# Second layer of the paired expert tiles: sums taken from PSUM, and three of four Strassen sums moved behind the scatter

## The chip, the cores and the metric

The kernel runs on one core of one Trainium2 chip. The metric is the device time of one execution in microseconds (us). Before the change three runs gave 2141.28, 2142.96 and 2143.67 us, a median of 2142.96 us. The profiled execution, from which all durations below are taken, took 2142.86 us; the part of it that the profile covers (its span) is 2140.9 us.

## The reference, cut to what matters

The model block is a cross attention (32 samples, 112 tokens of 256 features, 375 context rows) followed by a mixture of 8 experts. The change touches only the mixture's second layer. Its reference, shortened:

```python
xf = x.reshape(T, D)                                   # T = 3584 tokens, D = 256
gate_scores = softmax(xf @ gate_w)                     # 8 experts
topk_scores, topk_idx = top_k(gate_scores, 2)          # two experts for each token
topk_scores = topk_scores / sum(topk_scores)
h = gelu(einsum('td,edf->etf', xf, w1) + b1[:, None])  # F = 1024
y = einsum('etf,efd->etd', h, w2) + b2[:, None]
out = einsum('kt,ktd->td', topk_scores.T, y[topk_idx.T, tok])
x = x + tanh(g_ffn) * out
```

Everything is in float32. The kernel computes each token only for its two experts.

## The kernel before, in words

**Stages.** Up to about 1705 us the kernel does the attention and, for each finished slab of 128 tokens, routes the tokens: it writes each token's normalised row twice (once for each expert) into a DRAM buffer `xg` sorted by expert. From about 1705 to 2006 us it works through that buffer in *pairs*, 256 rows of one expert at a time (two blocks of 128 rows, b = 0 and 1). Rows that do not fill a pair are done from 1988 us to the end in *singles* of 128 rows, with plain products. This text deals with the pairs, t = 0 to 20. Pair 0 is done plainly; pairs 1 to 20 use a Strassen-Winograd scheme: the 2x2 block product of (rows) x (weights) needs 7 block products in place of 8, at the price of sums and differences of blocks before and after.

**One iteration, in the order in which the loop (L1563 to L1585) issues it.** All five engines run lists written out in this order (`tc.manual_schedule`), so each engine meets its own instructions in exactly this sequence:

1. `hidden_pair(t)`: seven products of the first layer, each of 8 matmuls (L1057), in the order 1, 6, 7, 5, 4, 2, 3, into tiles of the PSUM pool `ps_m`, which has 4 buffers. ScalarE copies product 1 (L1067); VectorE adds the other products into the tile `h` with seven adds, L1068, L1069, L1071, L1072, L1073, L1075 and L1076; ScalarE applies gelu (L1064).
2. `fetch_first(t + 1)`: SyncE issues the loads of the next pair's first-layer weights (L934). Each weight tile has one buffer, so that a load waits for the products of pair t that read it. The loads are conditional: they are left out when pair t + 1 has the same expert as pair t.
3. `turn_rows(t + 1)`: TensorE transposes the next pair's rows (L969) into a `ps_m` tile, ScalarE copies it to `xsT` (L973).
4. `rows_sums(t + 1)`: four GpSimd sums of 128x128 (L985) for the next pair's first layer.
5. `pieces_of(6)`: up to six pieces of leftover routing work, mostly on VectorE; it is used up by pair 8.
6. `hidden_sums(t)`: the four GpSimd sums of 128x512 for the second layer of pair t (L1094 and L1095): v0 = a21 + a22, a21 = a11 - a21 in place, v1 = v0 - a11, v2 = a12 - v1.
7. `second_pair(t - 1)`: seven products of the second layer of the pair in front (L1114), four into the PSUM tile `ps_ya`, which read a11, a12, a22 and v0, then three into `ps_yb`, which read a21, v1 and v2. ScalarE makes the scaled bias `by` (L1128) and copies the whole of `ps_ya` to the SBUF tile `q` (L1130). VectorE forms the result `y` from `q` and `ps_yb` in six adds (L1131, L1134 to L1138) and two multiply-adds, one for each block (L1140).
8. `out_pair(t - 1)`: GpSimd issues two indirect DMAs (L1018) that add the rows of `y` to the output in DRAM, one for each block. The last sum (v2, L1095) stands between the two.
9. `fetch_second(t)`: SyncE issues the loads of the second-layer weights of pair t (L951), which wait for the products of pair t - 1; then `fetch_rows(t + 3)` (L881) and, while there are any, one routing scatter to `xg` on GpSimd (L682).

Two facts of this order matter. VectorE meets the `y` adds of pair t - 1 just before the first-layer adds L1068 to L1076 of pair t + 1. And since `ps_m` has four buffers, used in the order of the products, product 2 takes the buffer of product 6, which is free once L1068 has run, and the transpose takes that of product 5, free once L1072 has run.

Of the kernel before, what the change touches and what calls it, by code (L numbers as in the profile page):

```python
# [8 lines left out]
F32 = mybir.dt.float32  # L9
I32 = mybir.dt.int32  # L10
AF = mybir.ActivationFunctionType
ALU = mybir.AluOpType
# [11 lines left out]
def kernel(  # L24
# [20 lines left out]
    nc = tc.nc  # L45

    P = 128
# [69 lines left out]
    for e in range(E):  # L117
# [35 lines left out]
    sums = {  # L153
        tag: [const.tile([P, E + 4], F32, name=f"sums{tag}_{n}") for n in range(4)] for tag in "abc"
    }
# [19 lines left out]
    if True:  # L175
# [641 lines left out]
        found = {}  # L817
# [54 lines left out]
        xs, xsT, xt, hid, hs, psy, ys, wt, bias = {}, {}, {}, {}, {}, {}, {}, {}, {}  # L872
# [143 lines left out]
        def add_rows(t, b, y):  # L1016

            add = nc.gpsimd.indirect_dma_start(  # L1018
                out=outf,
                out_offset=bass.IndirectOffsetOnAxis(  # L1020
                    ap=xs[t][:, b, D + 1 : D + 2].bitcast(I32), axis=0
                ),
                in_=y,
                in_offset=None,
                compute_op=ALU.add,
            )
            if b == 0 and "loose" in found:

                tc.add_manual_dep(
                    add.ins,  # L1030
                    found.pop("loose").name,
                    mybir.DependencyInfo(mybir.DependencyClass.Sync, mybir.DependencyReason.DATA),
                    reason="the same tokens",
                )
            return add

        def combine(t):
            n = 2 if t == 0 else 1
            y = found["tiles"].tile([P, 2, D], F32, tag="y", name=f"y_{t}")
            for b in range(n):  # L1040
                nc.vector.tensor_tensor(y[:, b], psy.pop((t, b)), bias[t][1], ALU.add)
                nc.vector.tensor_scalar(y[:, b], y[:, b], xs[t][:, b, D : D + 1], None, ALU.mult)  # L1042
                add_rows(t, b, y[:, b])


        def hidden_pair(t):


            h = hid[t] = found["tiles"].tile([P, NF, 2, P], F32, tag="h", name=f"h_{t}")
            x, v = xsT[t], xt[t]  # L1050
            H = NF // 2
            h11, h12, h21, h22 = (h[:, i : i + H, b, :] for i in (0, H) for b in range(2))

            def product(n, w, r):
                ps = ps_m.tile([P, H, P], F32, tag="m", name=f"ps_h_{t}_{n}")
                for c in range(H):
                    nc.tensor.matmul(  # L1057
                        ps[:, c, :], lhsT=wt[w][:, c * P : (c + 1) * P], rhs=r, start=True, stop=True
                    )
                return ps  # L1060

            def gelu(lo):
                for f in range(lo, lo + H):
                    nc.scalar.activation(h[:, f], h[:, f], AF.Gelu, bias=bias[t][0][:, f : f + 1])  # L1064

            add = nc.vector.tensor_tensor
            nc.scalar.copy(h11, product(1, "11", x[:, 0, 0]))  # L1067
            add(h12, product(6, "s2", v[:, 1]), h11, ALU.add)  # L1068
            add(h21, product(7, "s3", v[:, 2]), h12, ALU.add)  # L1069
            ps = product(5, "s1", v[:, 0])  # L1070
            add(h22, ps, h21, ALU.add)  # L1071
            add(h12, ps, h12, ALU.add)  # L1072
            add(h21, product(4, "22", v[:, 3]), h21, ALU.add)  # L1073
            gelu(H)
            add(h11, product(2, "12", x[:, 1, 0]), h11, ALU.add)  # L1075
            add(h12, product(3, "s4", x[:, 1, 1]), h12, ALU.add)  # L1076
            gelu(0)

        def hidden_sums(t):


            h, H = hid[t], NF // 2
            v = hs[t] = [
                found["tiles"].tile([P, H, P], F32, tag=f"hs{n}", name=f"hs{n}_{t}", bufs=1)
                for n in range(3)
            ]
            a11, a12, a21, a22 = (h[:, i : i + H, b, :] for b in range(2) for i in (0, H))
            sub = ALU.subtract
            for o, l, r, op in (
                (v[0], a21, a22, ALU.add),  # L1090
                (a21, a11, a21, sub),
                (v[1], v[0], a11, sub),
            ):
                nc.gpsimd.tensor_tensor(o, l, r, op)  # L1094
            last = lambda: nc.gpsimd.tensor_tensor(v[2], a12, v[1], sub)  # L1095
            if t > 1:
                found["last_sum"] = last
            else:
                last()

        def second_pair(t):


            h, v, H = hid[t], hs[t], NF // 2
            a11, a12, a21, a22 = (h[:, i : i + H, b, :] for b in range(2) for i in (0, H))
            b21, b22 = (wt["b2x"][:, :, i * P : (i + 1) * P] for i in range(2))
            tiles = found["tiles"]

            def products(name, parts):
                ps = ps_s.tile([P, 2, 512], F32, tag="s", name=f"ps_{name}_{t}")[:, 0, :]  # L1110
                ps = ps.rearrange("p (n d) -> p n d", d=P)
                for n, (w, r) in enumerate(parts):
                    for c in range(H):
                        nc.tensor.matmul(  # L1114
                            ps[:, n, :],
                            lhsT=w[:, c, :],
                            rhs=r[:, c, :],
                            start=(c == 0),
                            stop=(c == H - 1),
                        )  # L1120
                return ps

            y = tiles.tile([P, 2, D], F32, tag="y", name=f"y_{t}")
            q = tiles.tile([P, 4, P], F32, tag="q", name=f"q_{t}", bufs=1)
            u = tiles.tile([P, 2, P], F32, tag="u", name=f"u_{t}", bufs=1)
            by = tiles.tile([P, 2, D], F32, tag="by", name=f"by_{t}", bufs=1)
            for b in range(2):
                nc.scalar.mul(by[:, b], bias[t][1], xs[t][:, b, D : D + 1])  # L1128
            ps = products("ya", ((a11, wt["b11"]), (a12, b21), (a22, wt["t4"]), (v[0], wt["t1"])))
            nc.scalar.copy(q, ps)  # L1130
            nc.vector.tensor_tensor(y[:, 0, :P], q[:, 0], q[:, 1], ALU.add)  # L1131
            ps = products("yb", ((a21, wt["t3"]), (v[1], wt["t2"]), (v[2], b22)))
            add = nc.vector.tensor_tensor
            add(u[:, 0], ps[:, 1], q[:, 0], ALU.add)  # L1134
            add(u[:, 1], ps[:, 0], u[:, 0], ALU.add)
            add(y[:, 1, :P], u[:, 1], q[:, 2], ALU.add)
            add(y[:, :, P:], u, q[:, 3].unsqueeze(1).to_broadcast([P, 2, P]), ALU.add)
            add(y[:, 0, P:], ps[:, 2], y[:, 0, P:], ALU.add)  # L1138
            for b in range(2):
                nc.vector.scalar_tensor_tensor(  # L1140
                    y[:, b], y[:, b], xs[t][:, b, D : D + 1], by[:, b], ALU.mult, ALU.add
                )
            found["rows_out"] = y

        def out_pair(t):

            y = found.pop("rows_out")
            one = add_rows(t, 0, y[:, 0])
            last_sum = found.pop("last_sum", None)
            if last_sum:  # L1150
                last_sum()
            other = add_rows(t, 1, y[:, 1])
            if last_sum:
                tc.declare_no_dep(other.ins, one.ins, reason="rows of other tokens")
                found["loose"] = one.ins

# [147 lines left out]
        def do(parts):  # L1304
            for part in parts:
                part()
# [13 lines left out]
        ps = ps_m.tile([P, 4 * KD], F32, tag="m", name="ps_ln")  # L1320
# [53 lines left out]
        for n in range(LAST):  # L1374
# [46 lines left out]
            if nb < B:  # L1421
# [12 lines left out]
                if m in (6, 7) and nb + 2 < B or n == 1:  # L1434
                    u = m - 4 if m > 1 else 1
# [103 lines left out]
        r, _ = route_parts(g, nc.vector)  # L1539
# [23 lines left out]
        for t in range(1, PAIRS):  # L1563
            hidden_pair(t)
            fetch_first(t + 1)
            turn_rows(t + 1, nc.scalar.copy if t > 1 else None)
            if t + 1 < PAIRS:
                rows_sums(t + 1)
            pieces_of(6)
            hidden_sums(t)  # L1570
            if t > 1:
                second_pair(t - 1)
                out_pair(t - 1)
                fetch_second(t)
            else:
                second_plain(1)
                combine(0)
            if t + AHEAD == EARLY:
                pieces_of(len(todo))
                do(outgoing)  # L1580
                del outgoing[:]
            fetch_rows(t + AHEAD)
            if outgoing:
                outgoing.pop(0)()
# [65 lines left out]
```

## Time and profile before

| what | before |
|---|---|
| median of 3 runs | 2142.96 us |
| profiled execution | 2142.86 us, span 2140.9 us |
| TensorE busy | 2090.6 us, 98% of the span |
| VectorE busy | 1392.8 us, 65% |
| ScalarE busy | 1199.6 us, 56% |
| GpSimd busy | 963.3 us, 45% |
| `y` adds L1136, 128x128 | 20 times; 291 ns shortest, 1344 ns median, 1364 ns longest |
| `y` adds L1137, 128x256 | 20 times; 413 ns shortest, 1483 ns median, 1489 ns longest |
| `y` adds L1134, 128x128, one input in PSUM | 20 times; 279, 292 and 293 ns |
| copy of `ps_ya`, L1130, 128x512 | 20 times; 567 ns median |
| GpSimd sums L1094, 128x512 | 1262 to 1317 ns median |
| scatter L1018 on GpSimd | 60 times; 1552 ns median; 4.0, 5.7 and 7.8 us from issue to landing |

The engines in the profile are PE (TensorE's matmuls), PEld (its weight loads, which overlap the matmuls), DVE (VectorE), ACT (ScalarE), POOL (GpSimd) and SPq (SyncE's queue, which issues loads). In a timeline row the columns are the start in us from the beginning of the span, the length in us, engine, line of the kernel, operation, output and inputs, and in square brackets how long the engine had been idle and what ended that. In the list of waits a row says which engine and line waited for which, then the total in us, how often, and the longest.

### The profile page before, as it was taken

The numbers are of one execution on the slowest core, as the hardware profiler recorded it, in microseconds if no ns is written. First come the engines' busy times: TensorE is split into PE (matmuls) and PEld (weight loads), VectorE is DVE, ScalarE is ACT, GpSimd is POOL, SyncE is SP. The second block draws the span as 40 slices with busy tenths as digits, with TensorE's granted clock in tenths as the row PEclk, the third lists the DMA queues.
The fourth block names the chain that finished last, engine by engine and source line by source line (L and its number), as shares of the span: only waits on it lengthen the run. The fifth ranks groups of instructions, "written<-read, shape, count | busy, mean of one in ns | idle before, by whom it ended". The sixth has DMA issues, their size and how long they took to land. (4 is left out here: it accounts for less than half of the span.)

```text
span 2140.9 us, 44362 instructions
## 1 busy us (share of the span) xinstructions
PE 2090.6 (98%) x16232; PEld 1645.9 (77%) x16232; DVE 1392.8 (65%) x2985; ACT 1199.6 (56%) x2817; POOL 963.3 (45%) x1412
## 2 busy tenths in 40 slices
PE   9999999999999999999999999999999998999998
PEld 5777777777777777777777777777777888988887
DVE  6667676767676767676767676766767478666211
ACT  5666565656665666656666666665655443433433
POOL 4432323343345645553536443643323286766312
PEclk9999999999999999999999999999999999999999
DMA  6693000010012212222112211210002476598773
GB/s 149 187 319 103 18 13 18 13 30 18 18 44 63 67 55 58 61 67 58 55 55 65 65 55 55 68 54 6 6 6 73 134 196 179 161 298 267 191 212 64
DMA packets 201027, 193.89 MB, mean 91 GB/s; under 512 B 25856, under 2 KB 170824, under 8 KB 200680
## 3 DMA queue, kind: packets, MB, share of 16 engines
q1 hardware_dynamic: 188344, 174.65, 27.4%
q0 software_dynamic: 11328, 15.33, 3.8%
q8 instruction: 130, 2.13, 0.4%
q10 hardware_dynamic: 1136, 1.05, 0.2%
q14 instruction: 89, 0.73, 0.1%
HBM read 168.20 MB, written 65.76 MB: 109 GB/s over the span
## 5 line engine op out<-in xcount | busy, mean ns | idle before, releaser
L492 ACT ACTIVATE ex<-ex,rc 112x487 f32<-112x487 f32 x512 | 331.1, 694 | 329.4 <-DVE rc L490 326.4
L468 DVE TENSOR_REDUCE nmx<-ps_s 112x2 f32<-112x974 f32 x256 | 288.0, 1167 | 311.5 <-PE ps_s L458 310.5
L478 ACT ACTIVATE ex<-ps_s,nmx 112x487 f32<-112x487 f32 x512 | 337.1, 666 | 159.8 <-DVE nmx L468 157.4
L499 PEld LDWEIGHTS ps_t<-ident,ex 112*122 112x122 f32 x2048 | 231.9, 138 | 120.1 <-issue 96.4
L499 PE MATMUL ps_t<-ident,ex 112*122 112x112 f32 x2048 | 280.8, 259 | 1.0 <-ACT h L1001 1.0
L403 POOL TENSOR_TENSOR vv<-tmpv,vv 122x512 f32<-122x512 f32 x64 | 81.3, 1270 | 416.2 <-ACT vv L421 333.0
L503 DVE COPY exT<-ps_t 122x448 f32<-122x448 f32 x384 | 237.4, 618 | 36.1 <-PE ps_t L499 35.0
L458 PE MATMUL ps_s<-kT,qT 64*112 64x487 f32 x1024 | 242.0, 591 | 0.0
L513 PEld LDWEIGHTS ps_o<-exT,vv 122*64 122x64 f32 (+1 forms) x4096 | 197.6, 136 | 44.8 <-DVE kT L417 33.0
L513 PE MATMUL ps_o<-exT,vv 122*64 122x112 f32 (+1 forms) x4096 | 211.4, 260 | 0.0
L393 PE MATMUL ps_v<-wkv_s,tT 128*122 128x128 f32 x1536 | 202.3, 275 | 1.2 <-DVE vv L417 1.2
L403 POOL TENSOR_TENSOR kT<-tmpk,kT 128x487 f32<-128x487 f32 x63 | 76.8, 1220 | 270.6 <-ACT kT L421 270.6
L387 PE MATMUL ps_k<-tT,wkv_s 128*128 128x487 f32 x378 | 189.4, 583 | 4.2 <-ACT qT L326 3.5
L393 PEld LDWEIGHTS ps_v<-wkv_s,tT 128*122 128x122 f32 x1536 | 181.9, 185 | 4.2 <-DVE vv L417 1.8
L393 PEld LDWEIGHTS ps_v<-wkv,kvT 128*122 128x122 f32 x1024 | 125.9, 185 | 74.3 <-issue 56.7
L1018 POOL DMA_INDIRECT out_dram<-y,xs x60 | 93.4, 1557 | 144.6 <-DVE y L1042 89.4
L427 DVE TENSOR_TENSOR kT<-ps_k,kT 128x487 f32<-128x487 f32 x189 | 124.7, 660 | 48.2 <-PE ps_k L387 41.9
L427 DVE TENSOR_TENSOR vv<-ps_v,vv 122x512 f32<-122x512 f32 x192 | 131.6, 685 | 35.4 <-PE ps_v L393 29.9
L458 PEld LDWEIGHTS ps_s<-kT,qT 64*112 64x112 f32 x1024 | 81.1, 172 | 79.5 <-issue 63.2
L393 PE MATMUL ps_v<-wkv,kvT 128*122 128x128 f32 x1024 | 139.0, 279 | 1.0 <-DVE kT L427 1.0
L1064 ACT ACTIVATE h<-h,b 128x256 f32<-128x256 f32 x160 | 66.0, 495 | 129.2 <-DMA b<-b1d 59.2
L387 PE MATMUL ps_k<-kvT,wkv 128*128 128x487 f32 x252 | 130.2, 598 | 0.0
(288 smaller groups left out, 4018.4 us busy)
## 6 DMA issues: line engine op xcount, KB each, us to landing
w<-in_L_ffn_w_dram SPq DMA_DIRECT2D x132, 256.0 KB
xg<-pad SPq DMA_DIRECT2D x8, 3640.0 KB
w_s<-ws SPq DMA_DIRECT2D x80, 256.0 KB
w_t<-ws SPq DMA_DIRECT2D x80, 256.0 KB
w_b2x<-in_L_ffn_w_dram SPq DMA_DIRECT2D x38, 512.0 KB
piece<-in_L_ffn_w_dram SPq DMA_DIRECT2D x128, 128.0 KB
ws<-piece SPq DMA_DIRECT2D x256, 64.0 KB
cin<-in_ctx_dram SPq DMA_DIRECT2D x32, 336.0 KB
```

Source lines behind the costliest of these rows:

```text
L387: nc.tensor.matmul(ps, lhsT=w[:, 0, i * P : (i + 1) * P], rhs=x[:, :NK], start=True, stop=True)
L393: nc.tensor.matmul(ps[:, c, :], lhsT=x[:, c * KC : (c + 1) * KC], rhs=w[:, 1, i * P : (i + 1) * P], start=True, stop=True,)
L403: nc.gpsimd.tensor_tensor(v[o], v[l], v[r], ALU.add)
L427: nc.vector.tensor_tensor(v[at], product(n, w, x), v[at], ALU.add)
L458: nc.tensor.matmul(ps[:, j, :NK], lhsT=qT[b // 2, i][r, b % 2, :], rhs=kT[b, i][r, :], start=True, stop=True,)
L468: nc.vector.tensor_reduce(nmx[b, i], pss[b, i][:, :, :NK], AX.X, ALU.max, negate=True)
L478: nc.scalar.activation(t[:, j, :NK], ps[:, j, :NK], AF.Exp, bias=nmx[b, i][:, j : j + 1], accum_out=sm[b, i][:, j : j + 1],)
L492: nc.scalar.mul(ex[b, i][:, j, :NK], ex[b, i][:, j, :NK], rc[:, j : j + 1])
L499: nc.tensor.transpose(ps[:, c, :], ex[b, i][:, j, c * KC : (c + 1) * KC], ident[:S, :S])
L503: (nc.scalar.copy if h == 2 else nc.vector.tensor_copy)(exT[b, i, j], ps)
L513: nc.tensor.matmul(ps[y * DH : (y + 1) * DH, r, x * S : (x + 1) * S], lhsT=vv[j][:m, c, x, r, y * DH : (y + 1) * DH], rhs=exT[2 * g + x, i ...
L1018: add = nc.gpsimd.indirect_dma_start(out=outf, out_offset=bass.IndirectOffsetOnAxis(ap=xs[t][:, b, D + 1 : D + 2].bitcast(I32), axis=0), i ...
```

## The change

It makes two edits, for pairs 1 to 20.

First, in `second_pair`, only the first of the four products in `ps_ya` is copied to SBUF (`q` is 128x128 in place of 128x512). The other three are read by VectorE from PSUM where they are. The adds stay the same in number and size; L1131, L1136 and L1137 now have one input in PSUM.

Second, of the four GpSimd sums of `hidden_sums` only v0 stays where it was. The difference in place (a21) moves between the two scatters of the pair in front, where v2 was, and v1 and v2 move behind the second scatter. For pair 1 the three follow the two scatters of pair 0.

```diff
@@ hidden_sums
-            for o, l, r, op in (
-                (v[0], a21, a22, ALU.add),
-                (a21, a11, a21, sub),
-                (v[1], v[0], a11, sub),
-            ):
-                nc.gpsimd.tensor_tensor(o, l, r, op)
-            last = lambda: nc.gpsimd.tensor_tensor(v[2], a12, v[1], sub)
-            if t > 1:
-                found["last_sum"] = last
-            else:
-                last()
+            nc.gpsimd.tensor_tensor(v[0], a21, a22, ALU.add)
+
+
+            found["sums"] = [
+                lambda o=o, l=l, r=r: nc.gpsimd.tensor_tensor(o, l, r, sub)
+                for o, l, r in ((a21, a11, a21), (v[1], v[0], a11), (v[2], a12, v[1]))
+            ]
@@ second_pair
-            q = tiles.tile([P, 4, P], F32, tag="q", name=f"q_{t}", bufs=1)
+            q = tiles.tile([P, P], F32, tag="q", name=f"q_{t}", bufs=1)
...
             ps = products("ya", ((a11, wt["b11"]), (a12, b21), (a22, wt["t4"]), (v[0], wt["t1"])))
-            nc.scalar.copy(q, ps)
-            nc.vector.tensor_tensor(y[:, 0, :P], q[:, 0], q[:, 1], ALU.add)
-            ps = products("yb", ((a21, wt["t3"]), (v[1], wt["t2"]), (v[2], b22)))
             add = nc.vector.tensor_tensor
-            add(u[:, 0], ps[:, 1], q[:, 0], ALU.add)
-            add(u[:, 1], ps[:, 0], u[:, 0], ALU.add)
-            add(y[:, 1, :P], u[:, 1], q[:, 2], ALU.add)
-            add(y[:, :, P:], u, q[:, 3].unsqueeze(1).to_broadcast([P, 2, P]), ALU.add)
-            add(y[:, 0, P:], ps[:, 2], y[:, 0, P:], ALU.add)
+            nc.scalar.copy(q, ps[:, 0])
+            add(y[:, 0, :P], ps[:, 1], q, ALU.add)
+            ps_ = products("yb", ((a21, wt["t3"]), (v[1], wt["t2"]), (v[2], b22)))
+            add(u[:, 0], ps_[:, 1], q, ALU.add)
+            add(u[:, 1], ps_[:, 0], u[:, 0], ALU.add)
+            add(y[:, 1, :P], ps[:, 2], u[:, 1], ALU.add)
+            add(y[:, :, P:], ps[:, 3].unsqueeze(1).to_broadcast([P, 2, P]), u, ALU.add)
+            add(y[:, 0, P:], ps_[:, 2], y[:, 0, P:], ALU.add)
@@ out_pair
             one = add_rows(t, 0, y[:, 0])
-            last_sum = found.pop("last_sum", None)
-            if last_sum:
-                last_sum()
+            sums = found.pop("sums", [])
+            do(sums[:1])
             other = add_rows(t, 1, y[:, 1])
-            if last_sum:
+            do(sums[1:])
+            if sums:
                 tc.declare_no_dep(other.ins, one.ins, reason="rows of other tokens")
                 found["loose"] = one.ins
@@ the loop over pairs, t = 1
                 second_plain(1)
                 combine(0)
+                do(found.pop("sums"))
```

## The prediction

> **What bounds the kernel now.** I began with the page: TensorE is busy 98% of the span, so time can only come from gaps on TensorE.
>
> ```profile
> PE 2090.6 (98%) x16232; PEld 1645.9 (77%) x16232; DVE 1392.8 (65%) x2985; ACT 1199.6 (56%) x2817; POOL 963.3 (45%) x1412
> ```
>
> Then the list of waits over the pairs (1705 to 2010 us), for what TensorE waited on there. It is VectorE's first-layer adds, nearly once a pair, each time for a PSUM buffer:
>
> ```profile
> PEld ps_h L1057 <- DVE h L1068: 21.2, 17, 2.2
> PE ps_h L1057 <- DVE h L1068: 18.0, 17, 2.1
> PE ps_x L969 <- DVE h L1072: 3.7, 16, 0.2
> ```
>
> Why those adds are late is in the timeline of one pair (t = 11):
>
> ```profile
> 1843.05 1.06 PE L1057 MATMUL ps_h<-xsT,w 128*128 128x128 f32 x8
> ...
> 1843.25 0.29 DVE L1134 TENSOR_TENSOR u<-ps_yb,q 128x128 f32<-128x128 f32 x1 [1.03 <-PE ps_yb L1114]
> ...
> 1843.83 1.27 POOL L1094 TENSOR_TENSOR h<-h 128x512 f32<-128x512 f32 x1
> ...
> 1843.90 1.35 DVE L1136 TENSOR_TENSOR y<-u,q 128x128 f32<-128x128 f32 x1
> ...
> 1845.05 1.32 POOL L1094 TENSOR_TENSOR hs<-hs,h 128x512 f32<-128x512 f32 x1
> ...
> 1845.17 1.49 DVE L1137 TENSOR_TENSOR y<-u,q 128x256 f32<-128x256 f32 x1
> ...
> 1847.02 0.88 DVE L1140 SCALAR_TENSOR_TENSOR y<-y,xs,by 128x256 f32<-128x256 f32 x2
> ...
> 1847.78 1.57 POOL L1018 DMA_INDIRECT out_dram<-y,xs  x1 [1.41 <-PE ps_h L1057]
> 1847.81 0.69 DVE L1068 TENSOR_TENSOR h<-ps_h,h 128x512 f32<-128x512 f32 x1
> ...
> 1848.55 1.16 PE L1057 MATMUL ps_h<-xsT,w 128*128 128x128 f32 x8 [0.88 <-DVE h L1068]
> ...
> 1850.84 0.63 PE L969 MATMUL ps_x<-ident,xs 128*128 128x128 f32 x4 [0.23 <-DVE h L1072]
> ...
> 1857.55 0.83 PE L1057 MATMUL ps_h<-xsT,w 128*128 128x128 f32 x6
> ```
>
> L1136 and L1137 stretch until the GpSimd sum beside them ends (1843.83 + 1.27 = 1845.10, 1845.05 + 1.32 = 1846.37). Both read two SBUF tiles. The adds with one input in PSUM never stretch (L1134: 279 to 293 ns in all 20). So `y` is done at 1847.9, L1068 starts after it, and product 2 waits for L1068.
>
> TensorE's floor: its products start 0.893 us apart when nothing is in the way (1843.94 to 1846.62 is three). A pair is 14 products and a transpose of 0.46, so 12.96 us. This pair took 14.50: product 2 came 1.04 late, the transpose 0.40, and the product after a stop took 1.00 for 0.89.
>
> Last, the loads, from the busy time by stretch over pairs 13 to 19, where every pair has a new expert, and just behind:
>
> ```profile
> 1865.25:1966.75 101.50, 93.80 (x812) 91.34 (x812) 64.43 (x106) 39.44 (x91) 69.70 (x70) 1.00 0.99 296
> 1966.75:1974.00 7.25, 7.09 (x64) 7.12 (x65) 2.30 (x6) 5.05 (x12) 4.22 (x6) 1.00 0.40 71
> ```
>
> The last two columns are the DMA engines' busy share and GB/s: for seven pairs the DMA engines are already full at 14.5 us a pair.
>
> [...] 1.35 us for an add that takes 0.29 alone, ending as the sum ends. [...]
>
> **The change, part by part.**
>
> *Adds from PSUM.* L1136 and L1137 can't be locked out any more. Their price unlocked is 0.29 and 0.42 (shortest of their rows; [...] I take the rows, as L1134 and L1138 read PSUM at 0.29). This takes 1.06 + 1.07 = 2.1 us off the VectorE chain in front of L1068. L1131 the same, but it sits in idle time. L1140 still has two SBUF inputs; under a sum it took 2.45 us for the two in pair 4, in place of 0.88.
>
> *Sums moved.* Beside the `y` adds GpSimd now only waits for `y`, so L1140 stays at 0.88. New chain from the last product's end, at 0.20 after the pair's first matmul: 0.33 + 0.32 + 0.33 + 0.44 + 0.33 + 0.88 = 2.6, so L1068 runs from 2.8 to 3.5. Product 2 wants its buffer after five products, 4.47: 0.9 to spare. L1072 ends by about 5.2, the transpose wants it at 6.25. Both stalls go: 14.50 to 12.96, **1.54 a pair**.
>
> *The copy cut to a quarter.* 567 ns now[...]. It is hidden: L1130 ended at 1856.38, 1.4 us before L1134 wanted `q`. Worth nothing[...].
>
> *The new places on GpSimd's queue.* The scatter that waits for `y` now has three sums and the next pair's L985 queued behind it, and TensorE waits for all of these. Counted from the pair's first matmul: `y` of block 0 at about 2.4, scatter 1.57, a21 1.27, scatter 1.57, v1 and v2 2 x 1.27, gaps of 0.17: done at 9.7. The products that need a21, v1, v2 start at 10.3, 11.2 and 12.1, so with 2.4 to spare or more. Behind v2 stand a routing scatter (1.0 and 0.3 gap, in eight early pairs) and the four L985, which want `xsT` (ready about 10.1) and end at 12.0 to 12.8; product 6 of the next pair needs the second of them at 13.85. v0 then ends at about 14.1, 1.1 into the next pair, before L1140 at 1.7. Both scatters go out earlier than before; nothing else on SyncE's or GpSimd's queue is passed. PSUM: `ps_ya` is held until 1.6 into the next pair, and is written again at 6.7.
>
> *Pairs 2 and 3.* For pair 0 the second scatter waits for the first to land (1716.65 to 1721.38, 4.7 us). The three sums of pair 1 now stand behind it: scatter at 1712.8, second at 1717.5, then a21, v1, v2 until 1723.0, while product a21 would want its input at 1719.5. A **new wait** of about 2 us that eats what L1068 frees there (1.9). GpSimd reaches the L985 of pair 3 at 1724.3 as before, and the existing wait on it stays. Gain 0.
>
> *Pairs 7 and 8.* Here routing pieces hold VectorE up to 3.3 us into the pair (L1131 at 1785.92 and 1801.56), so the `y` chain wasn't stretched at all in pair 7. They are the bound; I take 1.2 and 0.6 of excesses of 2.7 and 3.9 (pair 8 also has a granted clock of 0.90).
>
> Sum by pair, period less 12.96: 2 and 3: 0; 4: 1.9; 5: 1.5; 6: 1.5 of 2.5 (0.9 is a gap at the routing counts); 7: 1.2; 8: 0.6; 9: 0.4 of 13.41; 10 to 19: 15.4; 20: 1.3. **23.8 us.**
>
> *Loads.* Over pairs 13 to 19 30.0 MB must move; packet time is 0.99 x 101.5 = 100.5 us. The fullest stretches of 7.25 us show a share of 1.04, so these loads take at least 96.6 us. They are issued from 4.5 us into pair 12's iteration (1862.08 of 1857.55[...]), and the last is wanted 11.2 into pair 19's, so TensorE at its floor leaves 7 x 12.96 + 11.2 - 6.5 = 95.4 us. Short by 1.2; with a share of 1.02, by 3. I take **2 lost**. Nothing stops TensorE on loads there today, so this is a bound that only appears.
>
> 23.8 - 2 = 21.8 off the profiled 2142.86: **2121 us**; the median shown is 0.1 higher, no difference.
>
> **Rivals.**
> *Loads become the bound outright.* For: 0.99 share already. Against: 0.40 right behind, and loads that are not wanted at once. If pairs 13 to 19 stay near 14.2 (0.99/1.02 of 14.5), they gain 0.3 each and not 1.54, less 9: 15 off, 2128.
> *More than summed.* Pairs 6 to 8 and the clock dip in 8 come right too: 5 more, and no loss on loads: 2114.
> *Nothing.* Were the adds not freed by PSUM inputs (some other cause of the stretch), the moved sums alone still clear them; so no gain needs both reasons to be wrong: 2143.
> *Slower: the second scatter waits for the first to land.* It does so for pair 0, at 4.7 us. If the declared independence failed for the other pairs with the sums moved, GpSimd's loop (`y`, scatter, landing, scatter, v1, v2, products, `y`) would be 2.6 + 0.2 + 7.4 (median landing in pairs 13 to 19) + 1.6 + 2.6 + 0.9 and gaps of 0.4: 15.7 against 14.5, 1.2 on some 17 pairs, 2163. It decides once landing takes over 6.2. Against: before, the second scatter starts 0.17 behind v2, without waiting, and the declaration stands.
>
> **How the numbers follow.** Forecast (2116 to 2126) 0.62; loads bound (2126 to 2133) 0.17; more (2108 to 2116) 0.10; nothing 0.04; slower 0.07. 0.2% (4.3 us) is about what a measurement can tell. Faster 0.89, same 0.04, slower 0.07. The range of 8 in 10 takes the forecast, most of the loads case and half of "more": 2112 to 2132.
>
> **What would show it.** Right: L1136's and L1137's successors at about 0.29 and 0.42 in all 20; waits on L1068 nearly gone; first products 13.0 apart in pairs 10 to 12; in pair 2 a wait of the yb products on GpSimd. In pairs 13 to 19 waits of TensorE for DMA of w, w_s, w_t, or none. Wrong, if yb products wait for GpSimd in every pair, or if the period holds at 14.5 with the adds short.

## The result, and the profile after

The changed kernel takes 2118.06 us, the median of four runs (2116.77 to 2118.73), against 2142.94 us for the kernel before, run beside it. The ratio is 0.9884, with a 95% interval of 0.9867 to 0.9901: 24.9 us, or 1.2%, faster. The profiled execution took 2118.11 us with a span of 2116.3 us, so the span lost 24.6 us.

Where they went can be read from the starts of each pair's first product, in the timeline of TensorE. From the start of pair 2 to the end of pair 20 the time went from 279.5 to 252.7 us, a loss of 26.8 us. Ahead of pair 2 the changed kernel is 0.7 us later, and behind pair 20, in the singles, it takes 1.5 us more. These two vary from one execution to the next: in a second profile of the same changed kernel (one of the experiments below) pair 2 starts 0.2 us earlier than before the change, and the singles take 0.1 us more. The length of the pairs in us:

| pair | 2 | 3 | 4 | 5 | 6 | 7 | 8 | 9 | 10 to 19, mean | 20 |
|---|---|---|---|---|---|---|---|---|---|---|
| before | 14.88 | 14.10 | 14.88 | 14.50 | 15.48 | 15.69 | 16.84 | 13.41 | 14.51 | 14.65 |
| after | 15.34 | 13.81 | 12.94 | 12.95 | 13.61 | 13.30 | 15.64 | 12.94 | 12.94 | 12.73 |

From the page of the changed kernel, the busy time of each engine and its share of the span. TensorE has the same 16232 matmuls and is still busy for 98%; VectorE has 24.9 us less of busy time in the same number of instructions:

```profile
PE 2084.2 (98%) x16232; PEld 1644.0 (78%) x16232; DVE 1367.9 (65%) x2985; ACT 1194.0 (56%) x2817; POOL 965.8 (46%) x1412
```

From the list of waits of the changed kernel over the pairs and the first singles (1705 to 2010 us): which engine and line waited for which, the total in us, how often, and the longest:

```profile
PE ps_h L1057 <- DVE h L1068: 2.7, 2, 2.0
...
PE ps_y L1175 <- DMA w_b1x<-in_L_ffn_w_dram: 1.5, 1, 1.5
...
PEld ps_yb L1110 <- POOL hs L1093: 1.4, 4, 0.5
```

The wait on L1068 was 18.0 us in 17 pairs; it is left in two. The transpose's wait on L1072 went from 3.7 to 0.8. Two rows of this kind are new: four short waits of a second-layer product for a GpSimd sum, and one of a single for its weights (0.4 us in the second profile).

The timeline of pair 11 of the changed kernel (start, length, engine, line, operation, output and inputs, idle time ahead of it and what ended that). Line numbers have moved by four: L1132 and L1133 are the adds that were L1136 and L1137, L1136 is the multiply-add that was L1140, and L1089 and L1093 are the GpSimd sums.

```profile
1832.92 1.06 PE L1057 MATMUL ps_h<-xsT,w 128*128 128x128 f32 x8
...
1833.11 1.27 POOL L1089 TENSOR_TENSOR hs<-h 128x512 f32<-128x512 f32 x1
...
1833.78 0.29 DVE L1132 TENSOR_TENSOR y<-ps_ya,u 128x128 f32<-128x128 f32 x1
...
1834.76 0.88 DVE L1136 SCALAR_TENSOR_TENSOR y<-y,xs,by 128x256 f32<-128x256 f32 x2
...
1835.52 1.57 POOL L1018 DMA_INDIRECT out_dram<-y,xs  x1 [1.14 <-DVE y L1136]
1835.55 0.68 DVE L1068 TENSOR_TENSOR h<-ps_h,h 128x512 f32<-128x512 f32 x1
...
1838.57 1.57 POOL L1018 DMA_INDIRECT out_dram<-y,xs  x1 [0.16 <-DVE h L1072]
...
1845.87 1.06 PE L1057 MATMUL ps_h<-xsT,w 128*128 128x128 f32 x8
```

The sum v0 (L1089) still runs beside the add L1132, from 1833.11 to 1834.38, and L1132 takes 0.29 us all the same, with one of its inputs in PSUM. While the multiply-adds run, GpSimd only waits for `y` (1.14 us). L1068 ends 3.3 us into the pair, where product 2 wants it at 4.5, and the next pair starts 12.95 later. The second scatter does not wait for the first to land.

By source line, the least, median and greatest time in ns of the two adds:

```profile
L1132 DVE TENSOR_TENSOR y<-ps_ya,u x20: 290/291/292, 1727.1 to 1973.9; 128x128 f32<-128x128 f32 x20
...
L1133 DVE TENSOR_TENSOR y<-ps_ya,u x20: 411/411/416, 1727.3 to 1974.1; 128x256 f32<-128x256 f32 x20
```

Not one add in 20 is stretched; the medians were 1344 and 1483 ns. The longest multiply-add takes 494 ns, and the copy to `q` 246 ns in the median. In the second profile v0 ran late in pairs 6 and 11, and there one multiply-add took 927 and one 718 ns (482 in the median of the first profile; 1479 at the longest before the change): with two inputs in SBUF, it is out of the way of the sums only as long as v0 ends early enough.

Last, the busy time of the engines over seven of the pairs that each have a new expert (the stretch and its length, then TensorE, its weight loads, VectorE, ScalarE, GpSimd, and at the end the granted clock, the DMA engines' share and GB/s):

```profile
1852.00:1945.00 93.00, 93.00 (x836) 93.00 (x835) 50.42 (x107) 39.62 (x97) 72.09 (x72) 1.00 1.04 327
```

TensorE is busy for all of the 93 us. The loads of this stretch were all hidden, at a share of 1.04, so a share of one is not the ceiling.

### The profile page after: what moved, and what is told of

It reads as the page before. It is cut to its first block, busy times and chain, and to the rows that moved or that the text cites. A ratio compares the mean times of both kernels' runs of the same rounds, so it can differ in the third digit from the quotient of the medians.

```text
span 2116.3 us, 44362 instructions
## 1 busy us (share of the span) xinstructions
PE 2084.2 (98%) x16232; PEld 1644.0 (78%) x16232; DVE 1367.9 (65%) x2985; ACT 1194.0 (56%) x2817; POOL 965.8 (46%) x1412
## 5 line engine op out<-in xcount | busy, mean ns | idle before, releaser
L1243 POOL TENSOR_TENSOR piece<-piece 128x128 f32<-128x128 f32 x256 | 120.0, 469 | 16.5 <-DMA piece<-in_L_ffn_w_dram 2.5
```

The source lines that it names most:

```text
L1243: nc.gpsimd.tensor_tensor(o, l, r, op) for o, l, r, op in ops
```

## The experiments

The theory was that GpSimd's sums hold up VectorE's adds with two SBUF inputs, that this is all that made L1068 late, and that behind it TensorE's own floor decides. The rivals: that only one of the two edits does the work; that the shorter copy has a part; that the loads are the next bound; and that, if the scatters had to land in turn, the moved sums would cost more than they save. Each kernel was timed beside runs of the kernel before on the same chip.

**Each edit alone.** The first one leaves the sums where they were and only reads the products from PSUM:

```diff
 # before, second_pair
-            nc.scalar.copy(q, ps)
-            nc.vector.tensor_tensor(y[:, 0, :P], q[:, 0], q[:, 1], ALU.add)
+            nc.scalar.copy(q, ps[:, 0])
+            add(y[:, 0, :P], ps[:, 1], q, ALU.add)
...
-            add(y[:, 1, :P], u[:, 1], q[:, 2], ALU.add)
-            add(y[:, :, P:], u, q[:, 3].unsqueeze(1).to_broadcast([P, 2, P]), ALU.add)
+            add(y[:, 1, :P], ps[:, 2], u[:, 1], ALU.add)
+            add(y[:, :, P:], ps[:, 3].unsqueeze(1).to_broadcast([P, 2, P]), u, ALU.add)
```

> The first edit alone: adds read PSUM, the four sums stand as before. Theory 1 (the stretch is GpSimd's sums[...]): L1136 and L1137 fall from 1344 and 1483 ns to 291 and 411, but the multiply-adds for y still have two SBUF inputs and now meet the sums, so they stretch from 0.88 us a pair to some 1.7 to 2.4; the add for product 6 then ends about 4.0 to 4.9 into the pair, at the edge of the 4.47 at which product 2 wants its buffer. A pair takes 12.95 to 13.4, and the kernel 2117 to 2127 us. Theory 2 (the order of the sums is what counts, the adds were not the cause): it stays near 2143.

Measured: 2127.08 us against 2144.69, ratio 0.9915 (0.9901 to 0.9928). Pairs 12 to 19 take 13.38 or 13.39 us. The pair part is 15.2 us shorter, of the 26.8 that both edits bring. The adds are short in all pairs (medians 291 and 411 ns). But the stretch has moved on, to the multiply-adds. By source line, and then the timeline of one pair of this kernel:

```profile
L1140 DVE SCALAR_TENSOR_TENSOR y<-y,xs,by x40: 473/485/1495, 1726.1 to 1985.8; 128x256 f32<-128x256 f32 x40
```

```profile
1868.15 1.89 DVE L1140 SCALAR_TENSOR_TENSOR y<-y,xs,by 128x256 f32<-128x256 f32 x2
...
1868.29 1.47 POOL L1094 TENSOR_TENSOR hs<-hs,h 128x512 f32<-128x512 f32 x1
```

The two multiply-adds take 1.89 us beside the third sum, where they take 0.88 alone, and L1068 starts behind them, at 1869.96. They read `y` and `by`, both in SBUF, and `y` can't be left in PSUM by this edit. The sum is held up as well, 1.47 us in place of 1.27. So 0.44 of the pair's 1.57 us stay lost.

The second one takes the changed kernel and puts back the old `second_pair`: the whole of `ps_ya` is copied, the adds read two SBUF tiles, and only the sums are moved. The two adds that matter, out of that edit:

```diff
 # after, second_pair
-            add(y[:, 1, :P], ps[:, 2], u[:, 1], ALU.add)
-            add(y[:, :, P:], ps[:, 3].unsqueeze(1).to_broadcast([P, 2, P]), u, ALU.add)
+            add(y[:, 1, :P], u[:, 1], q[:, 2], ALU.add)
+            add(y[:, :, P:], u, q[:, 3].unsqueeze(1).to_broadcast([P, 2, P]), ALU.add)
```

> The second edit alone: three sums stand behind the first scatter, all four products are copied, adds read SBUF. Theory 1[...]: with no sum beside them the adds fall to 291 and 411 ns though both inputs are in SBUF; a pair takes 12.95 to 13.2, and the kernel 2116 to 2121 us. Theory 3 (adds with two SBUF inputs are slow in this stage whatever GpSimd does): they stay at 1344 and 1483 ns, and the kernel near 2143.

Measured: 2121.01 us against 2144.69, ratio 0.9890 (0.9874 to 0.9905); the pair part is 23.1 us shorter. Pairs 12 to 18 take 12.94 like those of the changed kernel; pairs 2 to 7 and 9 to 11 take 0.2 to 0.8 us more than there. By source line, and in the timeline of an early pair:

```profile
L1132 DVE TENSOR_TENSOR y<-u,q x20: 291/292/1286, 1725.9 to 1976.5; 128x128 f32<-128x128 f32 x20
```

```profile
1739.41 1.26 POOL L1089 TENSOR_TENSOR hs<-h 128x512 f32<-128x512 f32 x1
...
1739.70 1.13 DVE L1132 TENSOR_TENSOR y<-u,q 128x128 f32<-128x128 f32 x1
```

With two SBUF inputs the add takes 292 ns in the median, as with one in PSUM; an add from SBUF is not slow in itself. It stretches to over 1 us in six pairs, 4 to 6 and 9 to 11, just those in which v0 still runs beside it, and ends within 0.2 us of it (1740.83 and 1740.67); in pairs 13 to 20 v0 has ended some 0.7 us before the add starts. Putting the operand in PSUM and putting the sum elsewhere are two ways to end the same stretch. They overlap: 15.2 and 23.1 alone, 26.8 together. (Of the 23.1 and of the 26.8, 1.2 are the granted clock in pair 8, see below; with the first edit alone it was 0.90 there, as before the change.)

**The shorter copy.** The changed kernel, with all four products copied and only the first of them read:

```diff
-            nc.scalar.copy(q, ps[:, 0])
-            add(y[:, 0, :P], ps[:, 1], q, ALU.add)
+            nc.scalar.copy(q, ps)
+            add(y[:, 0, :P], ps[:, 1], q[:, 0], ALU.add)
```

> The changed kernel, but all four products are copied to SBUF again (128x512) and only the first is read from there. Forecast step: the copy is hidden, 567 ns for 246 and no change, 2118 us within 2. Rival: the copy is on the path through the adds, 0.32 us a pair on 19 pairs, 2124.

Measured: 2116.76 us against 2144.69, ratio 0.9869 (0.9854 to 0.9884). The copy took 567 ns in place of 246, and pairs 9 to 19 still took 12.94 or 12.95. It is hidden, and its cut is worth nothing here.

**The wait in pair 2.** The second scatter of pair 0 waits for the first to land, and the change puts three sums behind that. Here they go between the two scatters:

```diff
 # in combine(t), after the scatter of block b
                 add_rows(t, b, y[:, b])
+                if t == 0 and b == 0:
+                    do(found.pop("sums"))
...
 # the loop over pairs, t = 1
                 combine(0)
-                do(found.pop("sums"))
```

> The changed kernel, but the three sums of pair 1 stand between the two scatters of pair 0, in the 4.7 us in which the second waits for the first to land. If the wait of pair 2 on these sums is what made its period 15.34 us, that falls to about 13.3 and the kernel takes 2116 us (2 less). Rival: the wait on the sums for the first layer of pair 3 takes its place, and nothing is gained, 2118.

Measured: 2116.64 us against 2144.69, ratio 0.9864 (0.9849 to 0.9879). Pairs 2 and 3 took 14.28 and 12.95 in place of 15.34 and 13.81, 1.9 us less. Pair 2 fell by less than I expected (13.3), since it keeps a wait of 0.65 us on L1068; pair 3 has the rest, as its wait for a GpSimd sum of the first layer (L985, 0.2 us) went too. The timeline of GpSimd, first of the changed kernel and then of the version with the sums between (columns as in the timeline above):

```profile
1713.63 1.70 POOL L1018 DMA_INDIRECT out_dram<-y,xs  x1 [0.44 <-DVE y L1042]
1718.24 1.56 POOL L1018 DMA_INDIRECT out_dram<-y,xs  x1 [2.91 <-DVE h L1075]
```

```profile
1712.11 1.70 POOL L1018 DMA_INDIRECT out_dram<-y,xs  x1 [0.44 <-DVE y L1042]
1713.28 1.84 POOL L1095 TENSOR_TENSOR h<-h 128x512 f32<-128x512 f32 x1
...
1717.87 1.57 POOL L1018 DMA_INDIRECT out_dram<-y,xs  x1 [0.16 <-issue]
```

The 2.91 us that GpSimd stood still are filled with the sums. The trace puts that wait down to VectorE's L1075, which the scatter doesn't need; with the sums in between, the second scatter starts 5.8 us after the first and waits for nothing, which fits the landing as its cause. The wait of pair 2's product for the sum (0.26 us in the changed kernel's timeline) is gone too.

The pair of kernels was run again side by side, unchanged:

> The changed kernel itself, on the same chip as its variant with the sums of pair 1 between the scatters of pair 0: 2118 us within 2.

> The sums of pair 1 between the two scatters of pair 0, as before, on the same chip as the changed kernel. The periods of pairs 2 and 3 added up to 27.2 us in place of 29.2 in its profile, so 2 us less than the changed kernel, 2116. Rival: the loads of the singles take the gain back, and no difference.

Measured, against 2142.73: 2117.23 us (2116.74 to 2118.84) for the changed kernel, ratio 0.9883 (0.9866 to 0.9899), and 2115.49 us (2113.04 to 2117.32) with the sums between, ratio 0.9876 (0.986 to 0.9893). The medians lie 1.7 us apart, but their runs overlap, so the times alone don't settle it; what is shown is that pairs 2 and 3 are shorter (14.27 and 12.94 again). The median with the sums between is the lowest of all that was run.

**The slower rival.** The changed kernel without the statement that the two scatters of a pair are independent, so that the second waits for the first to land in every pair:

```diff
             if sums:
-                tc.declare_no_dep(other.ins, one.ins, reason="rows of other tokens")
-                found["loose"] = one.ins
+                pass
```

> The changed kernel without the declaration that the two scatters of a pair are independent, so that the second waits for the first to land. Mechanism of the slower rival: first scatter 2.6 us into the pair, landing L after it, second scatter 1.6, v1 and v2 2.7, last product 0.9: a period of L + 7.9. With L = 5.7 (median over all) 13.6 us, with L = 7.4 (median where all weights are loaded) 15.3, where it is 12.95 now. The kernel takes 2135 to 2150 us, with waits of the yb products on GpSimd's sums in nearly every pair. Rival: GpSimd has so much room that the landing is hidden, 2118.

Measured: 2156.12 us against 2143.67, ratio 1.0059 (1.0043 to 1.0076): slower than before, and above the 2135 to 2150 that I expected of this run. From its list of waits over the pairs:

```profile
POOL out_dram L1018 <- DMA out_dram<-y,xs: 41.2, 11, 4.4
...
PE ps_yb L1110 <- POOL hs L1093: 22.2, 31, 2.2
```

The chain is the one that the prediction described: scatter, landing, scatter, v1 and v2, products. TensorE waits for the sums up to twice in a pair. Pairs 10 to 19 take 14.9 us in the mean, where the prediction worked out 15.7 from a landing of 7.4 us. But the landings of this run take 5.9 us in the median over these pairs, for which the formula above gives 13.8. Most of the 1.1 us between is a step that the formula leaves out: in pair 16 the first scatter lands after 5.8 us, and the second starts 6.6 us after the first. So the moved sums are a gain only because these scatters run one behind the other without waiting.

**Pair 7.** The two kernels with one edit each also tell what happened in pair 7, which went from 15.69 to 13.30 us: the PSUM edit alone leaves it at 15.69, the moved sums alone bring it to 13.59. I had taken the routing pieces that hold VectorE there as fixed. The timeline of the kernel before shows that they were stretched themselves:

```profile
1782.64 1.27 POOL L1094 TENSOR_TENSOR h<-h 128x512 f32<-128x512 f32 x1
1782.69 1.25 DVE L768 TENSOR_SCALAR wholeb<-restl 128x8 int32<-128x8 f32 x1
```

and that of the changed kernel, in which these sums run later:

```profile
1777.90 0.17 DVE L768 TENSOR_SCALAR wholeb<-restl 128x8 int32<-128x8 f32 x1
```

The one behind it, L771, ran beside the next sum and went from 1.19 to 0.17. Two instructions of 8 elements a partition took 2.4 us and take 0.3. That is 2.1 of the 2.4 us that pair 7 won. The changed kernel is not free of this: in their new places the sums meet other routing pieces, as here ahead of the `y` adds of pair 8, where L771, 0.17 us otherwise, is stretched:

```profile
1791.91 1.27 POOL L1089 TENSOR_TENSOR hs<-h 128x512 f32<-128x512 f32 x1
1792.08 1.14 DVE L771 TENSOR_SCALAR wholec<-wholec 128x8 int32<-128x8 int32 x1
```

**Routing pieces.** VectorE is busy 14.5 of the 15.64 us of pair 8, with routing pieces, and I took these for what keeps pairs 6 to 8 above the floor. One piece fewer in each pair:

```diff
-            pieces_of(6)
+            pieces_of(5)
```

> The changed kernel with five pieces of routing work a pair in place of six. If the 15.64 us of pair 8 come from the pieces in front of the adds for y on VectorE (product 2 waits 2.0 us there), pair 8 falls to 13.0 to 14.0, a later pair takes up to 1 us more, and the kernel takes about 2116 us. Rival: the long pair only moves to pair 9 or 10, 2118.

Measured: 2123.73 us against 2143.67, ratio 0.9906 (0.9889 to 0.9922). This expectation was missed. Pair 8 does fall, from 15.64 to 13.27, and pair 6 to 12.95. But the pieces that were put off come later, and hold up others. Pairs 10 to 12 take 15.05, 17.30 and 15.69. In pair 10 pieces stand ahead of the `y` adds again, and TensorE waits 1.4 us for L1068. Then the weights of pair 12 come late. The timeline of TensorE at its first product, and the longest wait of SyncE's queue over 1780 to 1860 us:

```profile
1848.54 2.05 PE L1057 MATMUL ps_h<-xsT,w 128*128 128x128 f32 x8 [4.19 <-DMA w<-in_L_ffn_w_dram]
```

```profile
SPq L881 <- DMA xg<-xr,sloti: 9.7, 1, 9.7
```

SyncE's queue stands for 9.7 us at the row load of pair 13 (L881), until the last routing scatter to `xg` has landed. GpSimd issues that scatter at 1841.25, and its last one in the changed kernel at 1830.29. The row load goes out at 1843.85 and the weights of pair 12 behind it, from 1845.82 on. That the scatter is late because of the pieces put off is argued from the order of the loop. Pair 12 itself has no wait: TensorE is busy for all of it, at a granted clock of 0.82.

Of pair 8, 1.2 us belong to neither kernel. By the busy time of that stretch, the granted clock was 0.90 before the change and 1.00 after it. The changed kernel, which was profiled twice, shows both for one and the same kernel: 15.64 us at 1.00 and 16.85 us at 0.90. So do two kernels that differ from it in other places: 15.63 us at 1.00 with the whole copy, 16.84 at 0.90 with the sums between.

**The loads.** How near are they to their limit? The first try added two, and then five, loads of 128 KB in each pair, all into one tile that nothing reads:

```diff
 # fetch_first, behind the loads of the first layer
+            if t < PAIRS:
+                for k in range(2):      # 5 in the second kernel
+                    nc.sync.dma_start(wt["more"], half_of_w1(e, k % 2, 1)[:, :256])
```

> The changed kernel with two more loads of 128 KB (rows of 1 KB, weights that are not used) in every pair[...]. Theory A (the forecast's: loads are at their limit in pairs 13 to 19, where packets already fill 1.04 of the engines' time): TensorE begins to wait for weights there, 1 to 5 us in all, 2119 to 2123. Theory B (they have room left): no wait, 2118.

> The changed kernel with five more loads of 128 KB in every pair[...]. Theory A (loads are at their limit): TensorE waits for weights 6 to 12 us in all, 2124 to 2130, in pairs 15 to 19 and not in the pairs that load little. Theory B: under 3 us, 2121 at most.

Measured: 2165.05 us, ratio 1.0101 (1.0084 to 1.0118), and 2292.24 us, ratio 1.0688 (1.067 to 1.0706). These say little of the limit, by an error of mine. Each load into the tile waits until the one before it has landed, and that wait sits on SyncE's queue ahead of the second-layer loads. From the list of waits of the kernel with two more:

```profile
SPq L937 <- DMA w_more<-in_L_ffn_w_dram: 53.1, 17, 5.2
```

TensorE in turn waited 19.7 us for the second-layer weights (11.5 for `w_b2x`, 8.2 for `w_b`). Not all of the loss is waiting: five pairs of this kernel had a granted clock of 0.82 to 0.91 (0.990 in the mean of the whole execution), and the second kernel had 0.965 in the mean, where the changed one has 0.998. What it does show: TensorE has no room for second-layer loads that are issued up to 5 us later. The second try copies 256 KB from DRAM to DRAM, once and three times in a pair, into places that nobody reads or waits for:

```diff
+            if t < PAIRS:
+                for k in range(1):      # 3 in the second kernel
+                    nc.sync.dma_start(spare[(1 * t + k) % 24], half_of_w1(e, k % 2, k // 2))
```

> The changed kernel with one more transfer of 256 KB in every pair, from a weight in DRAM to a DRAM buffer that nobody reads, so that it waits for nothing on its own account[...]. Theory A (loads are at their limit in pairs 13 to 19): TensorE waits for weights there, 3 to 5 us in all, 2121 to 2123. Theory B (the loads have room): no wait, 2118.

> Three such transfers in every pair[...]. Theory A: TensorE waits for weights 12 to 15 us in all in pairs 13 to 19, 2130 to 2133, and not in pairs with few loads. Theory B: 2121 at most.

Measured: one copy 2121.28 us, ratio 0.9902 (0.9886 to 0.9919); three copies 2141.83 us, ratio 0.9993 (0.9984 to 1.0002). The kernel before took 2142.73 us beside these and the changed one 2117.23. With one copy, pairs 2 to 13 keep their lengths within 0.21 us and pairs 14 to 19 take 13.0 to 13.6, 3.1 us more in all. With three, pairs 13 to 19 take 15.0 to 16.3. Busy time by stretch with one copy, and what TensorE waited for over pairs 13 to 19:

```profile
1852.00:1945.00 93.00, 91.20 (x808) 90.34 (x806) 49.58 (x106) 37.44 (x92) 69.74 (x71) 1.00 1.03 332
```

```profile
PE ps_h L1061 <- DVE u L1134: 1.5, 4, 0.4
PE ps_h L1061 <- DMA w<-in_L_ffn_w_dram: 0.3, 1, 0.3
```

TensorE is no longer busy throughout. It stops for 0.3 to 0.4 us at the first product of five pairs. The trace names a load of `w` once; L1134, named the other four times, gives nothing to that product, so I take it that these are loads as well. The rate went only from 327 to 332 GB/s although more was asked for. With three copies TensorE waits for second-layer loads, 8.9 us for `w_b2x` as below and 6.8 for `w_b`:

```profile
PE ps_ya L1114 <- DMA w_b2x<-in_L_ffn_w_dram: 8.9, 9, 1.9
```

So the changed kernel stands right at the edge of its loads in pairs 13 to 19: one more copy of 256 KB in a pair and they begin to cost. The one copy cost what I expected of it. The three cost some 25 us, where I expected 12 to 15, and only in pairs 13 to 19: there they cost 18.8, in pair 5 another 4.6 (2.5 us of waits for second-layer weights, and a granted clock of 0.90), and in pair 20 1.7.

What the edge is stays open. I took it for what the DMA engines can move, but each copy also takes a place on SyncE's queue, ahead of other loads. Over pairs 13 to 19 this queue waited, at the second-layer loads, for the `ps_yb` products that free their tiles: 20.9 us before the change, 6.2 after it, 2.3 with one copy and not at all with three. So it too has little room left. With one copy, the first-layer loads of pairs 15 to 19 go out 7.6 to 8.1 us into a pair in place of 6.4 to 6.9. No run here separates the two.

## Why the prediction was right, and where it was off

The forecast was 2121 us and the time 2118; it was right in the main mechanism and close in size. Two of its terms failed, those of pair 7 and of the loads, and both made the forecast too slow.

- *What bounded the kernel.* Right. The adds with two SBUF inputs were stretched by the sums beside them: 1344 and 1483 ns in the median before the change, 291 and 411 after it. The routing pieces of pair 7, with one tensor input each, were stretched in the same way (1247 and 1194 ns, 170 and 172 after the change). By what means a sum holds these instructions up, no run here shows. Both edits, each alone, end the stretch where they reach, and where they don't it stays: 1495 ns for a multiply-add, 1286 for an add. The rival that both reasons are wrong (2143) falls.
- *Adds from PSUM at 0.29 and 0.42.* Measured 291 and 411 ns, 292 and 416 at the longest. Reading PSUM costs the adds nothing that shows: from two SBUF tiles, with the sums alone moved, they take 292 and 418 in the median.
- *Floor of 12.96.* Measured 12.94 or 12.95 in 11 pairs on end.
- *1.54 a pair in pairs 10 to 19, 15.4 in all.* Measured 15.6.
- *L1068 done 3.5 into the pair, v2 at 9.7.* Measured in pair 11: 3.3 and 9.9. The new places on GpSimd's queue cost nothing in the steady pairs.
- *"Beside the `y` adds GpSimd now only waits for `y`."* Right in pairs 12 to 20, where v0 ends 0.1 us into the pair. In pairs 4 to 6 and 9 to 11 v0 ends at 1.2 to 2.1 (forecast: 1.1), so it does run beside them. There the PSUM inputs are what keeps the adds short, as the run with the sums alone shows.
- *The copy worth nothing.* Measured so: with 567 ns in place of 246, pairs 9 to 19 take the same 12.94 or 12.95 us.
- *Pairs 2 and 3: gain 0.* Off by little: pair 2 loses 0.46 and pair 3 wins 0.29. The new wait behind pair 0's scatter was there, and moving the sums in front of it brings 1.9 back. The old wait on L985 in pair 3 did not stay as it was: it fell from 0.9 to 0.2.
- *Pairs 6 and 7: 1.5 and 1.2.* Mis-sized: 1.9 and 2.4. That the routing pieces bind pair 7 was right; that they stay as long as they are was the step that failed: I looked for stretched instructions among the `y` adds alone. Two of the pieces were stretched by 2.1 us in all, and the moved sums freed them. For pair 6 I did not look for the 0.4.
- *Pair 8: 0.6.* Measured 1.2, all of it the clock of that execution: in the second profile pair 8 takes 16.85, as before the change. So nothing was won there.
- *Loads: 2 us lost in pairs 13 to 19.* The term that failed. Nothing was lost there. I had read the greatest share of a 7.25-us stretch in the kernel before, 1.04, as the limit, and worked out 96.6 us for these loads. But after the change the share is 1.04 over 93 us, and up to 1.09 in a stretch of 7.25 us. A share seen under less demand is a lower bound of the limit, not the limit. The real edge lies close by, as the extra copy shows, but the DMA engines need not be what sets it. The 6.5 us taken off in the 95.4 also held 2 us for a load to begin to move, an estimate of mine; the trace of the kernel before shows some 0.9 for a load of `b`: issued at 1859.56, and the DMA engines' share, 0.00 ahead of it, rises at 1860.4. A wait of the first single for its weights came up just behind (the row `ps_y <- DMA w_b1x`): 1.5 us in this profile and 0.4 in the second.
- *Pair 20: 1.3.* Measured 1.9. The rule of the sum, the length less 12.96, gives 1.7 here, and no reason stands beside the 1.3. The other 0.2 is that the transpose in pair 20 has 2 matmuls in place of 4, as a single follows; so its floor is lower.
- *A slip in a rival.* 0.99/1.02 of 14.5 is 14.1 and not 14.2, so that rival would come to 2127 in place of 2128.

The sum, in order: the pairs were forecast to bring 23.8 and brought 26.8 (of the 3.0 more, pair 7 has 1.2, pairs 8 and 20 have 0.6 each and pair 6 has 0.4); the loads were to take 2 back and took nothing in the pairs. The 1.5 in the singles and the 0.7 ahead of pair 2, in work that the change doesn't touch, differ in the second profile of the same kernel. There the pairs brought 25.1, as pair 8 had the lower clock again.

Of the rivals, "loads become the bound" named what comes next and put it too near by less than one copy of 256 KB a pair. "More than summed" was right in that pair 7 came nearly right too, and in that the pairs lose nothing on loads. The slower one has a mechanism that exists, as the run with waiting scatters shows, but the change doesn't set it off.

## What to carry to other kernels

Where VectorE and GpSimd work on SBUF at the same time, look at the longest of each group and not only at the mean: an operation that ends together with the other engine's, in many times its shortest time, may be held up by it, however small it is (here 1247 ns in place of 170). Here an operand in PSUM freed the adds (from 1344 ns in the median to 291), and another place in the other engine's list freed them as well (to 292); both were needed, as neither cleared every pair. Then look at what the moved operation runs beside in its new place. Before sums are moved behind a transfer on GpSimd's queue, find out what that transfer waits for, for here the same order with a landing in it is slower than the kernel before. And when the gain takes TensorE to its floor, ask which resource is next at its edge: here it was the loads or the queue that issues them, and a copy of 256 KB a pair was already too much.

## What was not expected of the hardware

An operation with one tensor of 8 elements a partition as its input was held up as the adds with two were (L768: 170 ns, or 1247 beside a GpSimd sum of 128x512). The multiply-add was expected to be, and was: 485 ns for 128x256 in the median, up to 1495 beside such a sum. The DMA engines' busy share rises above one, up to 1.09 in a stretch of 7.25 us (at 337 GB/s; another reached 360 at 1.04), and over 93 us 1.04 at 327 GB/s did not yet hold TensorE up; with more asked for, 332 GB/s was reached at a share of 1.03.
